# Bias vectors of folded weights: four column tiles and a second small matmul in place of full matmuls

## The chip, the cores and the metric

The kernel runs on one core of a Trainium2 chip. Its time is the device time of one execution in microseconds. The profile is one further execution, recorded by the hardware profiler. Engines are named as the profile names them: PE (matmuls) and PEld (weight loads), DVE (vector), ACT (activations), POOL (GpSimd), SP (issues most DMAs; a queue of an engine has a q behind its name).

## The reference

Two attention layers over a float32 image batch x of 8 x 512 x 32 x 32, so 8 images of 512 channels and 1024 tokens. Cut to what matters:

```python
# layer 0: eight heads of 64 channels, quantised q, k, v
h = group_norm(xf, gn_w, gn_b)                       # 32 groups
qkv = einsum('oc,bct->bot', qkv_w, h) + qkv_b
q, k, v = fake_quant(q), fake_quant(k), fake_quant(v)  # one scale each over the whole batch
w = softmax(einsum('bct,bcs->bts', q * scale, k * scale))
a = einsum('bts,bcs->bct', w, v)
x = xf + einsum('oc,bct->bot', proj_w, a) + proj_b
# layer 1: one head of 512 channels
t = group_norm(x, gn_w, gn_b) as tokens
q, k, v = t @ wq.T + bq, t @ wk.T + bk, t @ wv.T + bv
out = softmax(q @ k.T / sqrt(512)) @ v
x = x + out @ wp.T + bp
```

The kernel applies a norm's scale to x and leaves the norm's bias out of x. What that bias would have added after a linear layer is a constant vector, W times the norm's bias, and is added to the layer's own bias. Those vectors are what the change is about. The weights and biases are inputs, so they have to be computed on the chip in each execution.

## The kernel before

**First phase, about 0 to 628 us.** For each image b, x is loaded (`x`), normalised by DVE, and q, k, v are computed on PE with the weights `wqkv` (tiles `qkps` and `vps` in PSUM), evicted with their bias, tracked for minimum and maximum, and stored to DRAM (`q_d`, `k_d`, `v_d`). Image 0 is computed plainly; images 1 to 7 by a scheme of seven half-size products in place of eight (`qk_block`, `v_block`), for which sums of weights and tokens are kept. Here PSUM is one pool of eight banks (`one`).

The bias of q, k and v is made by `bias(i)`: `gbb` holds the norm's bias widened to 128 equal columns for each of the CC = 4 blocks e of 128 input channels. Four f32 matmuls with `gbb[:, e]` as weights and `wqkv[:, e, 512 columns]` as moving operand accumulate in one bank, in which all 128 rows are then equal: the vector lies along a row. For v that is the form wanted (`vb`). For q and k the vector is wanted by channel, one number per partition: `by_channel` multiplies each 128 x 128 block by the identity on DVE and sums each row (`qkb`). The three groups stand among image 0's matmuls: `bias(0)` after the third of its four channel blocks, `bias(1)` after the first k product, `bias(2)` after the first v product.

**Between the phases,** from the extrema of all images come the quantisation scales (`ext`, `exa` on POOL, `scl`, `rcp`, `bhi`). Meanwhile `fold()` starts on PE: it multiplies Wq by Wk and Wv by Wp of layer 1 (`wn`, loaded by `load_folded` into the tiles of tags h and v), 16 matmuls each, into `wa` and `wm`.

**Attention of image 0, from about 642 us.** A unit is a pair of heads, half of the 1024 queries and one block of 128 keys: two `st` matmuls, one exp on ACT (`pt`, six buffers), one sum `acc` on DVE, two `av` matmuls in column tiles of 64. A pair has 16 units, an image 64. At the end of a pair `row_sums` sums `acc` over the partitions with four column tiles of 32 (`sm`). The next pair's q, k and v are reloaded through `raw` (two buffers, SP queue) and quantised by DVE.

`fold()` is a generator; each step yields a weight, and the loop around it lets attention advance in proportion:

```python
for w in fold():
    folded += w
    while pos < (folded - F_FIRST) * A_IMAGE / F_FOLD:
        advance()
```

After the eight product steps come the bias steps. `gb` (for the scores of layer 1) is the folded Wq'Wk times layer 1's norm bias plus Wk' times bq; `ob` (for its output) is the folded Wv'Wp times the norm bias plus Wp' times bv, plus bp. For each, `weigh` runs two groups of four full matmuls into one bank `fold_b`: one over the folded matrix (`wa` or `wm`), one over `wn`, with `wide` (three biases, widened to 128 columns) as weights; then `by_channel`. Here the bank comes from a pool of two (`bank`). All matmuls are kept in program order on PE by `mm` (L96); on the other engines a scheduler orders the instructions when the kernel is built.

**The rest,** from about 776 us: for each image projection (`pj`), norm and layer 1, interleaved with the next image's attention.

Of the kernel before, what the change touches and what calls it, by code (L numbers as in the profile page):

```python
# [9 lines left out]
F32 = mybir.dt.float32  # L10
# [3 lines left out]
ALU = mybir.AluOpType  # L14
AX = mybir.AxisListType

P = 128
B, C, HH, WW = 8, 512, 32, 32
T = HH * WW
CC = C // P  # L20
# [3 lines left out]
PAIRS = HEADS // 2  # L24
# [16 lines left out]
V_GN0W, V_GN0B, V_PB0, V_GN1W, V_GN1B, V_BQ, V_BK, V_BP, V_BV, V_QKB = range(0, 40, 4)  # L41
# [3 lines left out]
WP0, WQ1, WK1, WV1, WP1, NQ1, NK1, NV1 = range(8)  # L45
# [3 lines left out]
def attn_pair_kernel(  # L49
# [9 lines left out]
    nc = tc.nc  # L59
# [10 lines left out]
    vec = const.tile([P, V_N], F32, name="vec")  # L70
    nc.scalar.dma_start(vec, vecs)
    ones = const.tile([P, P], F32, name="ones")
    nc.vector.memset(ones, 1.0)
    mhalf = const.tile([P, CC], F32, name="mhalf")
    nc.gpsimd.memset(mhalf, -0.5)

# [96 lines left out]
    with ExitStack() as fast:  # L173
# [7 lines left out]
        def bank(name):  # L181
            return ps_o.tile([P, 512], F32, tag="o", name=name)
# [35 lines left out]
        rs_d = [dram.tile([4, 512], F32, tag=f"rs{n}", name=f"rs_d{n}") for n in range(B * PAIRS)]  # L218
        rs1_d = [dram.tile([4, P], F32, tag=f"rs1{n}", name=f"rs1_d{n}") for n in range(B * NH)]

        def weigh(ps, terms):


            n = len(terms) * CC
            for i, (w, wide) in enumerate(terms):
                for e in range(CC):
                    mm(
                        ps.rearrange("p (a n) -> p a n", a=2), lhsT=wide[:, e, :], rhs=w(e),
                        start=(i == 0 and e == 0), stop=(i * CC + e == n - 1),
                    )  # L230
                yield 4.0

        def widen(dst, col):
            for e in range(CC):
                nc.vector.tensor_scalar(
                    dst[:, e, :], ones, vec[:, col + e : col + e + 1], None, ALU.mult
                )

        def by_channel(dst, ps):

            for e in range(CC):
                nc.vector.tensor_mul(ps[:, bass.ts(e, P)], ps[:, bass.ts(e, P)], ident)
            nc.vector.tensor_reduce(dst, ps.rearrange("p (e n) -> p e n", e=CC), AX.X, ALU.add)

        with tc.tile_pool(name="p1w", bufs=1) as p1w, tc.tile_pool(name="p1", bufs=3) as p1, tc.tile_pool(
            name="p1o", bufs=4
# [2 lines left out]
            def one(name):  # L249
                return ps_1.tile([P, 512], F32, tag="b", name=name)  # L250
# [216 lines left out]
            for i in range(2):  # L467
                nc.scalar.dma_start(vb[:, i, :], vbias[0:1, :].partition_broadcast(P))
            load_x(1)
            gbb = l1p.tile([P, CC, P], F32, tag="acc1", name="gbb")  # L470
            widen(gbb, V_GN0B)
            qkb = p1w.tile([P, 2 * PAIRS], F32, name="qkb")

            def bias(i):

                ps = one(f"bias{i}")
                w = wqkv[:, :, bass.ts(i, C)].rearrange("p e (a n) -> p e a n", a=2)
                for _ in weigh(ps, ((lambda e: w[:, e], gbb),)):
                    pass
                if i == 2:  # L480
                    for n in range(2):
                        nc.vector.tensor_add(vb[:, n, :], vb[:, n, :], ps)
                    return
                b4 = qkb[:, bass.ts(i, PAIRS)]
                by_channel(b4, ps)
                nc.vector.tensor_add(
                    b4, b4, vec[:, V_QKB + i * PAIRS : V_QKB + (i + 1) * PAIRS]
                )

            def qk_mm(b, ps, t, hf, cc):  # L490
# [8 lines left out]
            early = [[one(f"qkps_0_{t}_{hf}") for hf in range(NH)] for t in range(2)]  # L499
            for g in (*part, part[0], part[0], part[1]):  # L500
                next(g)
            then = iter((part[1], part[2], part[2], part[3], part[3]))
            for cc in range(CC):
                for t in range(2):
                    for hf in range(NH):
                        qk_mm(0, early[t], t, hf, cc)
                        if (cc, hf) in ((0, 1), (1, 0), (1, 1)):
                            next(next(then, iter(())), None)
                if cc == 2:
                    bias(0)  # L510
            load_x(2)
            ahead = prepare(1)
            more = weight_sums()
# [1 line left out]
            for t in range(2 * PAIRS):  # L515
                isk, j = divmod(t, PAIRS)
                if t < 2:
                    ps = early[t]
                else:
                    ps = [one(f"qkps_0_{t}_{hf}") for hf in range(NH)]  # L520
                    for hf in range(NH):
                        for cc in range(CC):
                            qk_mm(0, ps, t, hf, cc)
                if t == PAIRS:
                    bias(1)
                qk = p1o.tile([P, T], F32, tag="qk", name=f"qk1_0_{t}")
                mx, mn = (kmax, kmin) if isk else (qmax, qmin)
                for hf in range(NH):
                    nc.vector.tensor_scalar(
                        qk[:, bass.ts(hf, 512)], ps[hf], qkb[:, t : t + 1], None,  # L530
                        ALU.add, ALU.max, accum_out=column("kmax" if isk else "qmax", mx),
                    )
                nc.vector.tensor_reduce(mn[:, j : j + 1], qk, AX.X, ALU.min)
                nc.sync.dma_start((k_d if isk else q_d)[0][j], qk)
                if t > 0:
                    next(ahead, None)
            for t in range(NT):
                ps = one(f"vps_0_{t}")
                for cc in range(CC):
                    mm(  # L540
                        ps,
                        lhsT=hn[:, cc, bass.ts(t, P)],
                        rhs=wqkv[:, cc, 2 * C : 3 * C],
                        start=(cc == 0),
                        stop=(cc == CC - 1),
                    )
                if t == 0:
                    bias(2)
                vt = p1o.tile([P, 2, C], F32, tag="v2", bufs=3, name=f"v1_0_{t}")[:, 0, :]
                nc.vector.tensor_add(vt, ps, vb[:, 0, :])  # L550
                nc.vector.tensor_reduce(column("vmax", vmax), vt, AX.X, ALU.max)
                nc.vector.tensor_reduce(column("vmin", vmin), vt, AX.X, ALU.min)
                nc.sync.dma_start(v_d[0][:, t, :], vt)
                next(ahead, None)
                next(more, None)
# [733 lines left out]
        def fold():  # L1289


            wm = wm_tiles(0)

            def wa_rows(e):
                return wa[:, e // 2 : e // 2 + 3 : 2, e % 2, :]

            def wm_rows(e):
                return wm[e // 2][:, :, e % 2, :]

            for rows, lw, rw in ((wa_rows, NQ1, NK1), (wm_rows, NV1, WP1)):  # L1300
                for e in range(CC):
                    ps = bank(f"fold_{lw}_{e}")
                    for d in range(CC):
                        mm(
                            ps, lhsT=wn[lw][:, d, bass.ts(e, P)], rhs=wn[rw][:, d, :],
                            start=(d == 0), stop=(d == CC - 1),
                        )
                    nc.scalar.copy(rows(e), ps.rearrange("p (a n) -> p a n", a=2))
                    yield 4.0
            wide = l1p.tile([P, 3, CC, P], F32, tag="g", name="wide")  # L1310
            for i, col in enumerate((V_GN1B, V_BQ, V_BV)):
                widen(wide[:, i], col)

            def plain(i):
                w = wn[i].rearrange("p e (a n) -> p e a n", a=2)
                return lambda e: w[:, e]

            for i, (dst, w, w2) in enumerate(
                ((gb, wa_rows, plain(NK1)), (ob, wm_rows, plain(WP1)))
            ):  # L1320
                ps = bank(f"fold_b{i}")
                yield from weigh(ps, ((w, wide[:, 0]), (w2, wide[:, 1 + i])))
                by_channel(dst, ps)
            nc.vector.tensor_add(ob, ob, vec[:, V_BP : V_BP + CC])
            a11, a12, a21, a22, s1, s2, s4 = (wa[:, i] for i in range(7))
            tt(s1, a21, a22, ALU.add)
            tt(s2, s1, a11, ALU.subtract)
            tt(a21, a11, a21, ALU.subtract)
            tt(s4, a12, s2, ALU.subtract)
            (m11, m12), (m21, m22), (v1, v2), (v3, v4) = ([t[:, i] for i in range(2)] for t in wm)  # L1330
            tt(v1, m11, m12, ALU.subtract)
            tt(v2, m22, v1, ALU.subtract)
            tt(v3, m22, m12, ALU.add)
            tt(v4, m21, v2, ALU.subtract)
            for t, dst in zip(wm, wm_d):
                nc.sync.dma_start(dst, t)
# [24 lines left out]
        alone = True  # L1361
        att = attention()
        A_IMAGE = PAIRS * (NH * NT * 1.5 + 1.0)
        F_FOLD = 4.0 * (8 + 4)
        F_FIRST = 12.0
        pos, done = 0.0, 0
        dense = True
# [342 lines left out]
def _layout(i):  # L1710
# [12 lines left out]
    def col(v):  # L1723
# [14 lines left out]
            "L0_conv_proj_w", "L1_conv_wq", "L1_conv_wk", "L1_conv_wv", "L1_conv_wp",  # L1738
        )] + [wn(i[n]) for n in ("L1_conv_wq", "L1_conv_wk", "L1_conv_wv")]),
        "vecs": np.concatenate(vecs, axis=1),  # L1740
        "vbias": np.stack([qkv_b[:, 2].reshape(C), i["L1_conv_bv"]]),
    }


# [20 lines left out]
```

## Time and profile before

| | us |
|---|---|
| timed runs | median 2776.87 (2774.91 to 2778.79), three runs |
| profiled execution | 2774.02, span 2772.2 |
| PE busy in the span | 2714.3 (98%) |
| DVE busy | 1778.8 (64%) |
| ACT busy | 900.1 (32%) |
| `bias` matmuls, 24 passes | 592 ns each, from 33.5 to 91.9 |
| `fold_b` matmuls, 32 passes | 592 to 697 ns each, from 678.7 to 713.0 |

The profile lists an f32 matmul as two passes, so the twelve matmuls of `bias` are 24 rows. Passes are pipelined and overlap, so the time that a group takes from PE is read from the start of the group to the start of the next one, not from the sum of its durations. A row of the timeline reads: start, duration, engine, line, operation, output and inputs, shape, count, and in brackets how long the engine had been idle and who released it.

### The profile page before, as it was taken

To read this page: it belongs to the slowest core of one execution; us is meant where nothing else is said; L and a number is where in the kernel's file an instruction comes from. 1 tells how busy PE (TensorE), PEld (TensorE's weight loads), DVE (VectorE), ACT (ScalarE), POOL (GpSimd) and SP (SyncE) were. 2 spreads that over 40 slices of the span, in tenths; PEclk is the share of its full clock that TensorE was granted. 3 is DMA by queue.
4 is the path that set the end of the run, shared out by engine and by line. 5 is a ranking of instruction groups with operands and counts; after the bars stand their busy time and mean duration, and the time that the engine had idled before them with its cause. 6 is when DMAs were issued, how large, how long until landed. Compare 5 with 4: busy or idle time off the path is not lost.

```text
span 2772.2 us, 29206 instructions
## 1 busy us (share of the span) xinstructions
PE 2714.3 (98%) x11300; PEld 1646.7 (59%) x11300; DVE 1778.8 (64%) x2641; ACT 900.1 (32%) x1181; POOL 26.4 (1%) x28
## 2 busy tenths in 40 slices
PE   7999999999999999999999999999999999999998
PEld 3455555553236664665566556646664666467687
DVE  6666666547886667566766676666667566754544
ACT  0011111115644333433444244434443433443011
POOL 0000000000000000000000000000000000000000
PEclk9999999999999999999999999999999999999999
DMA  4323322135321232124212411231133124101301
GB/s 183 113 113 115 121 111 101 76 115 173 109 88 46 65 122 88 31 65 141 69 35 71 158 35 54 92 122 42 59 114 102 31 65 142 58 11 61 127 18 34
DMA packets 149094, 241.18 MB, mean 87 GB/s; under 512 B 24272, under 2 KB 89808, under 8 KB 147408
## 3 DMA queue, kind: packets, MB, share of 16 engines
q1 hardware_dynamic: 117424, 180.98, 19.6%
q10 hardware_dynamic: 31520, 58.23, 6.3%
q8 instruction: 90, 1.47, 0.2%
q14 instruction: 60, 0.49, 0.1%
HBM read 152.59 MB, written 86.28 MB: 86 GB/s over the span
## 4 chain that ended last, share of the span: by engine, by line
PE 77%; DVE 12%; DMA 6%; issue 2%; ACT 1%; POOL 1%; SPq 0%; ACTq 0%; DVEq 0%; POOLq 0%
PE qkps L96 12%; PE s L96 12%; PE av L96 12%; PE o L96 12%; PE pj L96 7%; PE v2ps L96 6%; PE vps L96 6%; PE g L96 5%; PE st L96 3%; DMA raw<-q_d 3%; DVE acc L752 3%; DVE acc L754 2%; PE sm L96 1%; ACT pt L743 1%; DVE h L145 1%
## 5 line engine op out<-in xcount | busy, mean ns | idle before, releaser
L743 ACT ACTIVATE pt<-st,esc 128x1024 f32<-128x1024 f32 x512 | 546.4, 1115 | 327.8 <-PE st L96 317.8
L96 PE MATMUL av<-pt,v 128*64 128x512 f32 x2048 | 476.5, 600 | 0.0
L752 DVE TENSOR_TENSOR acc<-acc,pt 128x1024 f32<-128x1024 f32 x254 | 310.6, 1223 | 117.6 <-ACT pt L743 108.1
L96 PEld LDWEIGHTS av<-pt,v 128*64 128x64 f32 x2048 | 132.0, 136 | 259.1 <-issue 258.7
L96 PE MATMUL s<-g,h 128*128 128x256 f32 x1024 | 236.5, 380 | 0.8
L96 PE MATMUL pj<-ao,wp 128*128 128x512 f32 x512 | 225.4, 596 | 7.5 <-DVE x L1126 3.6
L375 ACT ACTIVATE u<-qkps,qkb 128x512 f32<-128x512 f32 x84 | 57.7, 687 | 522.0 <-PE qkps L96 522.0
L96 PEld LDWEIGHTS s<-g,h 128*128 128x128 f32 x1024 | 193.5, 190 | 31.4 <-DVE v L1067 3.6
L96 PE MATMUL s<-g,sums 128*128 128x256 f32 x768 | 180.1, 384 | 4.1 <-DVE p L1082 3.4
L96 PEld LDWEIGHTS pj<-ao,wp 128*128 128x128 f32 x512 | 95.5, 190 | 131.4 <-issue 112.8
L754 DVE TENSOR_TENSOR acc<-acc,pt 128x1024 f32<-128x1024 f32 x130 | 158.5, 1219 | 21.7 <-ACT pt L743 18.0
L96 PE MATMUL o<-p,v 128*128 128x256 f32 x768 | 171.2, 379 | 0.0
L96 PEld LDWEIGHTS s<-g,sums 128*128 128x128 f32 x768 | 143.1, 190 | 36.9 <-issue 11.0
L96 PE MATMUL qkps<-x,wqkv 128*128 128x512 f32 x352 | 162.7, 606 | 2.3 <-DVE x L145 2.3
L96 PE MATMUL st<-q,k 64*128 64x512 bf16 x1024 | 157.0, 381 | 2.3 <-ACT pt L743 2.3
L96 PEld LDWEIGHTS o<-p,v 128*128 128x128 f32 x768 | 145.8, 190 | 20.1 <-issue 0.4
L96 PE MATMUL qkps<-sums,wa 128*128 128x512 f32 x336 | 153.3, 592 | 0.0
L96 PE MATMUL g<-h,wa 128*128 128x256 f32 x512 | 121.7, 385 | 12.2 <-DVE g L1025 11.4
L1082 DVE TENSOR_TENSOR p<-s,kept_u 128x512 f32<-128x512 f32 x90 | 61.8, 687 | 110.3 <-ACT kept_u L1049 102.2
L96 PEld LDWEIGHTS <-k 64*128 64x128 bf16 x1024 | 33.4, 94 | 164.7 <-issue 160.9
L96 PEld LDWEIGHTS g<-h,wa 128*128 128x128 f32 x512 | 94.7, 190 | 39.5 <-DVE g L1025 14.6
L96 PE MATMUL o<-g,vsum 128*128 128x256 f32 x512 | 117.2, 382 | 0.0
(210 smaller groups left out, 3358.5 us busy)
## 6 DMA issues: line engine op xcount, KB each, us to landing
x<-in_x_dram SPq DMA_DIRECT2D x32, 512.0 KB
raw<-q_d SPq DMA_DIRECT2D x32, 512.0 KB
raw<-k_d SPq DMA_DIRECT2D x32, 512.0 KB
raw<-v_d SPq DMA_DIRECT2D x32, 512.0 KB
rs<-rs_d SPq DMA_DIRECT2D x128, 128.0 KB
x_d<-h SPq DMA_DIRECT2D x64, 256.0 KB
x<-x_d ACTq DMA_DIRECT2D x64, 256.0 KB
out_dram<-x SPq DMA_DIRECT2D x64, 256.0 KB
```

Of the source, the lines that this page charges most:

```text
L96: ins = nc.tensor.matmul(*args, **kw).ins
L145: put(hf, lambda i=i, cc=cc, hf=hf: nc.vector.tensor_scalar(dst(cc, hf), src(cc, hf), mean[:, i : i + 1], rstd[:, i : i + 1], ALU.subtract ...
L375: nc.scalar.activation(dst, x, AF.Identity, bias=bias)
L743: nc.scalar.activation(pt, st, AF.Exp, scale=esc)
L752: later("sum", 0, lambda: nc.vector.tensor_add(acc, first, pt))
L754: nc.vector.tensor_add(acc, first, pt)
L1082: tt(dst, ps, u, ALU.add)
```

## The change

The vectors are computed in two steps. `weigh` runs the four blocks e as four matmuls of 32 weight columns each, each into its own 32 partitions of one bank (`wt`), so the four partial sums lie in four groups of 32 equal rows. ACT copies the bank to SBUF (`wsum` or `fold_room`). A second matmul with a constant `fourth` (4/128, a new tile) sums over the partitions: `by_channel` with four matmuls of one column (`wc`), which leaves the vector by channel, or `by_row` with one of 512 columns (`wr`) for v. The masking on DVE is gone.

In `fold()` the two steps over the folded matrices are gone. Instead DVE multiplies Wq and Wv of layer 1 with the norm's bias, loaded as a row (`gn1_row`, a third row of the input `vbias`), and sums (four instructions each, vector `z`), adds bq or bv, and widens that to 32 columns; `weigh` then runs over Wk or Wp alone. The second of the two `weigh` groups is followed by its reduction with nothing between. The weights of `fold()`'s steps sum to 34 in place of 48, so its steps fall differently between the units of attention.

```diff
+    fourth = const.tile([P, P], F32, name="fourth")
+    nc.gpsimd.memset(fourth, 4.0 / P)
...
-        def weigh(ps, terms):
-            n = len(terms) * CC
-            for i, (w, wide) in enumerate(terms):
+        def weigh(bank, room, w, wide, nm):
+            ps = bank(f"wt_{nm}")
+            for e in range(CC):
+                mm(
+                    ps[e * 32 : (e + 1) * 32, :], lhsT=wide[:, e, :], rhs=w(e),
+                    start=True, stop=True,
+                )
+            nc.scalar.copy(room, ps)
+            def by_channel():
+                tot = bank(f"wc_{nm}")[:, 0:CC]
                 for e in range(CC):
                     mm(
-                        ps.rearrange("p (a n) -> p a n", a=2), lhsT=wide[:, e, :], rhs=w(e),
-                        start=(i == 0 and e == 0), stop=(i * CC + e == n - 1),
+                        tot[:, e : e + 1], lhsT=room[:, bass.ts(e, P)], rhs=fourth[:, 0:1],
+                        start=True, stop=True,
                     )
-                yield 4.0
+                return tot
+            def by_row():
+                tot = bank(f"wr_{nm}")
+                mm(tot, lhsT=fourth, rhs=room, start=True, stop=True)
+                return tot
+            return by_channel, by_row
...
-        def by_channel(dst, ps):
-            for e in range(CC):
-                nc.vector.tensor_mul(ps[:, bass.ts(e, P)], ps[:, bass.ts(e, P)], ident)
-            nc.vector.tensor_reduce(dst, ps.rearrange("p (e n) -> p e n", e=CC), AX.X, ALU.add)
...
-                if cc == 2:
-                    bias(0)
+                if cc >= 2:
+                    next(bq, None)
...
-                if t == PAIRS:
-                    bias(1)
+                if t >= PAIRS - 1:
+                    next(bk, None)
+                if t == 2 * PAIRS - 1:
+                    next(bv)
...
+            row = l1p.tile([P, C], F32, tag="acc1", name="gn1_row")
+            nc.sync.dma_start(row, vbias[2:3, :].partition_broadcast(P))
+            wide = l1p.tile([P, 2, CC, 32], F32, tag="g", name="wide")
+            room = l1p.tile([P, C], F32, tag="rs1", name="fold_room")
+            for i, (w, w2, col) in enumerate(((NQ1, NK1, V_BQ), (NV1, WP1, V_BV))):
+                z = small.tile([P, CC], F32, tag="z", name=f"z{i}")
+                for e in range(CC):
+                    nc.vector.tensor_tensor_reduce(
+                        room, wn[w][:, e, :], row, 1.0, 0.0, ALU.mult, ALU.add,
+                        accum_out=z[:, e : e + 1],
+                    )
+                nc.vector.tensor_add(z, z, vec[:, col : col + CC])
+                widen(wide[:, i], z)
+            for i, (dst, w) in enumerate(((gb, NK1), (ob, WP1))):
+                by_channel, _ = weigh(
+                    bank, room, lambda e, w=w: wn[w][:, e, :], wide[:, i], f"f{i}"
+                )
+                yield 1.0
+                tot = by_channel()
+                if i == 0:
+                    nc.vector.tensor_copy(dst, tot)
+                else:
+                    nc.vector.tensor_add(dst, tot, vec[:, V_BP : V_BP + CC])
...
-        F_FOLD = 4.0 * (8 + 4)
+        F_FOLD = 4.0 * 8 + 2.0
```

More of the change, by code (lines that the diff above doesn't have):

```diff
@@ L235, in widen @@
                 nc.vector.tensor_scalar(
-                    dst[:, e, :], ones, vec[:, col + e : col + e + 1], None, ALU.mult
+                    dst[:, e, :], ones[:, 0:32], col[:, e : e + 1], None, ALU.mult
                 )
-        def by_channel(dst, ps):
-            for e in range(CC):
-                nc.vector.tensor_mul(ps[:, bass.ts(e, P)], ps[:, bass.ts(e, P)], ident)
-            nc.vector.tensor_reduce(dst, ps.rearrange("p (e n) -> p e n", e=CC), AX.X, ALU.add)
         with tc.tile_pool(name="p1w", bufs=1) as p1w, tc.tile_pool(name="p1", bufs=3) as p1, tc.tile_pool(
@@ L469, in attn_pair_kernel @@
             load_x(1)
-            gbb = l1p.tile([P, CC, P], F32, tag="acc1", name="gbb")
-            widen(gbb, V_GN0B)
+            gbb = l1p.tile([P, CC, 32], F32, tag="acc1", name="gbb")
+            widen(gbb, vec[:, V_GN0B : V_GN0B + CC])
             qkb = p1w.tile([P, 2 * PAIRS], F32, name="qkb")
             def bias(i):
[L476 to L479, printed above, removed]
+                by_channel, by_row = weigh(
+                    one, p1o.tile([P, 512], F32, tag="u4", bufs=1, name=f"wsum_{i}"),
+                    lambda e: wqkv[:, e, bass.ts(i, C)], gbb, f"{i}",
+                )
+                yield
                 if i == 2:
+                    tot = by_row()
                     for n in range(2):
-                        nc.vector.tensor_add(vb[:, n, :], vb[:, n, :], ps)
+                        nc.vector.tensor_add(vb[:, n, :], vb[:, n, :], tot)
                     return
-                b4 = qkb[:, bass.ts(i, PAIRS)]
-                by_channel(b4, ps)
                 nc.vector.tensor_add(
-                    b4, b4, vec[:, V_QKB + i * PAIRS : V_QKB + (i + 1) * PAIRS]
+                    qkb[:, bass.ts(i, PAIRS)], by_channel(),
+                    vec[:, V_QKB + i * PAIRS : V_QKB + (i + 1) * PAIRS],
                 )
@@ L501, in attn_pair_kernel @@
                 next(g)
+            bq, bk, bv = (bias(i) for i in range(3))
             then = iter((part[1], part[2], part[2], part[3], part[3]))
@@ L546, in attn_pair_kernel @@
                     )
-                if t == 0:
-                    bias(2)
+                next(bv, None)
                 vt = p1o.tile([P, 2, C], F32, tag="v2", bufs=3, name=f"v1_0_{t}")[:, 0, :]
@@ L1309, in fold @@
                     yield 4.0
[L1310 to L1324, printed above, removed]
+            row = l1p.tile([P, C], F32, tag="acc1", name="gn1_row")
+            nc.sync.dma_start(row, vbias[2:3, :].partition_broadcast(P))
+            wide = l1p.tile([P, 2, CC, 32], F32, tag="g", name="wide")
+            room = l1p.tile([P, C], F32, tag="rs1", name="fold_room")
+            sums_of = []
+            for i, (w, w2, col) in enumerate(((NQ1, NK1, V_BQ), (NV1, WP1, V_BV))):
[10 more added lines that the diff above has]
+                    bank, room, lambda e, w=w: wn[w][:, e, :], wide[:, i], f"f{i}"
+                )
+                yield 1.0
[4 more added lines that the diff above has]
+                    nc.vector.tensor_add(dst, tot, vec[:, V_BP : V_BP + CC])
             a11, a12, a21, a22, s1, s2, s4 = (wa[:, i] for i in range(7))
@@ L1740, in _layout @@
         "vecs": np.concatenate(vecs, axis=1),
-        "vbias": np.stack([qkv_b[:, 2].reshape(C), i["L1_conv_bv"]]),
+        "vbias": np.stack([qkv_b[:, 2].reshape(C), i["L1_conv_bv"], i["L1_conv_gn_b"]]),
     }
```

## The prediction

> **What bounds the kernel now.** I read the page's busy shares and its chain, then the busy time by stretch, then PE, DVE and SP in order of time where the bias matmuls stand, and last the chain of that part alone. Times "at 643" are microseconds from the start of the span of 2772.2.
>
> ```profile
> PE 2714.3 (98%) x11300; PEld 1646.7 (59%) x11300; DVE 1778.8 (64%) x2641; ACT 900.1 (32%) x1181; POOL 26.4 (1%) x28
> PE 77%; DVE 12%; DMA 6%; issue 2%; ACT 1%; POOL 1%; SPq 0%; ACTq 0%; DVEq 0%; POOLq 0%
> ```
>
> PE is the bound on average, but 12% of the chain is DVE and 6% DMA. By stretch (PE, PEld, DVE, ACT, POOL):
>
> ```profile
> 27.50:96.00 68.50, 68.50 (x160) 30.54 (x161) 51.68 (x110) 1.28 (x1) 1.95 (x2) 0.98 0.23 90
> 96.00:628.00 532.00, 530.51 (x1640) 308.82 (x1638) 334.29 (x650) 57.72 (x84) 6.05 (x6) 1.00 0.28 109
> 643.00:713.50 70.50, 70.50 (x278) 22.35 (x276) 56.30 (x64) 43.63 (x47) 0.00 (x0) 1.00 0.45 143
> 713.50:760.00 46.50, 42.49 (x205) 11.12 (x204) 42.58 (x48) 36.55 (x37) 0.00 (x0) 1.00 0.28 82
> ```
>
> The three `bias` groups lie in the first row, where PE never stops, and up to 628 it hardly does: what leaves PE there leaves the span. The four `fold_b` groups lie in the third row, PE full and DVE at 80%; in the fourth PE has 4 us of holes and DVE is at 92%. PE in order of time:
>
> ```profile
> 33.54 3.60 PE L96 MATMUL bias<-wqkv,gbb 128*128 128x512 f32 x8
> 36.97 11.32 PE L96 MATMUL qkps<-x,wqkv 128*128 128x512 f32 x26
> ...
> 708.88 1.06 PE L96 MATMUL sm<-acc,ones 128*32 128x512 f32 x8
> 709.88 3.70 PE L96 MATMUL fold_b<-wn_v,wide 128*128 128x512 f32 x8
> 713.51 0.61 PE L96 MATMUL st<-q,k 64*128 64x512 bf16 x4
> ```
>
> Start to start, four full f32 matmuls (eight passes) hold PE 36.97 - 33.54 = 3.43 us in the first phase and 713.51 - 709.88 = 3.63 us in attention. `sm` is already four column tiles of 32 side by side: 1.00 us. And the chain between 628 and 740, whose longest pieces are not PE's:
>
> ```profile
> 628.52 8.60 DMA k_d<-k
> 637.75 6.24 DMA raw<-v_d
> 673.03 5.80 DMA raw<-q_d
> 706.71 4.81 DMA raw<-q_d
> ```
>
> Beside PE runs a second chain there, of DVE and the reloads of `raw`, with next to no slack. So PE's gain there is not simply the span's.
>
> **What the Trainium skill says.** "TensorE: Matmul & The Clock Gate", Part 3, "Measured speedup vs the span model", has matmuls in different column groups run together: three tiles gave 2.38 times. The trace agrees: four `sm` tiles 1.00 us against 3.63, 3.6 times. "TensorEngine Tiling (Array Packing)", "Key Properties": changing the tiling mode drains the array. The trace has that inside `sm`'s 1.00 us, and the group after it loses nothing (3.63). The first page, "LDWEIGHTS (loading the stationary operand)", prices a load at its columns over 1.2 per ns, 107 ns for 128; the trace has 190 ns alone and 108 for 32 columns: the slope agrees, some 80 ns of latency come on top.
>
> **The change, part by part.**
>
> *First phase, PE.* Removed: three groups, 3 x 3.43 = 10.3. Added: three tile groups (`wt`) at the `sm` row's 1.00 = 3.0; for v one full matmul (`wr`), 3.43 / 4 = 0.86; for q and k four one-column matmuls each (`wc`). No row shows eight such weight loads in a row. Below: 8 x 107 ns = 0.9; above: 8 x 0.30, from `gps` on an idle PE, two passes in 0.59, = 2.4. I take 1.5, so 3.0 for both. Net 10.3 - 6.9 = 3.4. Each reduction waits for an ACT copy (0.59 as `wa<-fold`, once 1.28 for the table load, now first on ACT); in the built order 4 to 8 `qkps` or `vps` matmuls of 0.86 stand between, so it is hidden. A bias takes two of the eight PSUM banks in place of one, but `wt` leaves its bank to ACT at once, and PE wants no further bank for some 7 us. DVE loses the masking (two times 4 x 0.2 + 0.6) and evicts sooner; PE did not wait for that. The front order of DVE moves too: the normalisation of the second channel block comes about 1 us sooner by its rows (statistics of the fourth block fill a wait). PE stands 2.60 us for DVE before 27.22, so 0 to 1 of it; I take 0.5. Phase total 4 (2 to 5).
>
> *Hidden.* POOL: one memset (0.2, as `ident`) before `mhalf`, where POOL then sits idle 12. SP: `gn_row` stands before the store of `k_d` 3 and waits until `wt` 2 has read `gbb`, about 1 us after the store was ready; it and the v stores behind it only free buffers. DVE: eight multiply-and-sum instructions, each like `L350` 0.61 + 0.12 = 0.73. Four stand before the eviction that DVE waited 3.74 for at 620.56: 2.9 plus one add fit. Three, the add and four narrow widenings (together about 2.8) fit the 7.62 before `raw<-v_d` at 644.09. One stands ahead of the quantisation of `q_0` and `k_0` and waits for `wn_v`; its queue was empty at 636.6, the first half about 633, and PE needs `q_0` only at 642.5, when the first fold ends. The twelve wide widenings (0.2 each) go.
>
> *Attention of image 0.* Removed from PE: 4 x 3.63 = 14.5. Added: two `wt` 2.0, two `wc` 3.0. PE work falls by 9.5. With weights 34 for 48 the remaining folds sit later between units: after units 3, 7, 15 and 23 for 1, 3, 11 and 15. I walked PE, ACT, DVE and SP through the built order with these rows: st pair 0.53, av pair 1.87, exp 1.06, sum 1.13 to 1.23, quant 0.66, reload 4.4. Four things come out.
> 1. At the start `st` 2 and 3 now wait for the exps that the fold used to cover: about 1.6 of PE lost, and smaller waits later.
> 2. The DVE chain gains where the masking goes (1.94 at 699.7, 1.75 near 720) and where sums now fill its waits for `raw` (1.69 and 1.54).
> 3. A new wait: in the built order the last `wt`, `wc` follow each other. `wc` needs ACT's copy (0.8), and its bank (pool of two) only after DVE copies `gb`, which is queued on DVE behind four sums, the v quantisation and the `raw` reload. On PE everything stands behind it, first `st` of unit 36, then ACT. By the walk PE is ready at 707 and gets the bank at 709.4: a stand of 2 to 3.
> 4. `st` 36 starts at 710.6 for 713.5 (2.9 sooner), the sum over unit 36 at 712.2 for 720.6. Of those 8.4, 1.3 are two quants now still to do and 0.9 is masking that stood after it. After unit 36 DVE sets the pace: a pair of 16 units costs it 14 sums of 1.2, six quants of 0.66, 1.2 for `ao` and 0.25, 22.3 or 1.4 per unit, against PE's (0.53 + 1.87) / 2 = 1.2.
>
> So the stage ends about 7 sooner: at least 3 (PE's lead at unit 36, nothing more), at most 10 (all PE work, no stand). `h` now loads after the last `wt` of wn_h, some 5 later than before, and is first used at 776; the `wm_d` stores come later and are read an image later. From 776 the built order is the same, so the lead is kept.
>
> Sum: 4 + 7 = 11 against the profiled span 2772.2, whose run took 2774.02; the timed runs have a median of 2776.87 (2774.91 to 2778.79). The difference carries over to the median: 2766.
>
> **The rivals.**
> - *Attention gives its part back.* The DVE and reload chain (6.24, 5.80, 4.81 above) sets the stage's end and the new wait eats PE's lead; only the first phase and some masking remain: 4 + 1 = 5, time 2772, no measurable change. For it: the chain of 628 to 740. Against it: the chain itself loses 3.7 of masking and 3.2 of waits.
> - *All of PE's saving counts.* 3.4 + 9.5, weight loads at the low price (4 x 0.6 = 2.4), a front gain of 0.5: 15.8, time 2761. Against it: DVE at 92% in the fourth stretch.
> - *Slower: the tiles do not run side by side* with these operands, or each drains the array. Place: the five `wt` groups. A tile then costs a full matmul (0.86 or 0.91), 17.5 in place of 5; isolated `wc` cost 0.59 each, 9.4; `wr` 0.9 and the stand 3: 30.8 against 24.8 removed: 6 slower, 2783. It decides from a group of (5 + 11) / 5 = 3.2 us on. `sm` at 1.00, in f32 with 512 columns too, speaks against it.
> - *It does not do what it says:* the built order has the 32-row matmuls four by four, and the masking and `fold_b` groups are gone. Excluded.
>
> **How the numbers follow.** About 0.2% (5.5 us) is what a measurement of this kernel can tell from no change. Forecast 0.66, at 2766; part returned 0.16; all of it 0.11; slower 0.07. Faster is the forecast and all of it, 0.77; same 0.16; slower 0.07. The range reaches from all of PE's saving (2761) to between the returned case and no change (2774, a gain of 3: the low ends 2 + 3, less 2 for the spread of the runs); the slower case and a little of the returned one are outside.
>
> **What would show it.** Right: `wt` groups about 1.0 start to start, `wc` 0.9 to 2.4; PE without holes from 27 to 96, and the first fold about 4 sooner than 628.5; `q_0` and `k_0` ready before it ends; PE standing before the last `wc` with DVE or ACT as releaser; the first `pj` about 11 sooner than 776.0; from there to the end the same duration. Wrong: `wt` groups over 3 (the slower case); a fold that starts 4 sooner but a `pj` only 5 sooner (the returned case); a DVE wait on `wn_v` that PE's first fold does not cover; or a difference that arises after the first `pj`, for which I see no cause.

## The result and the profile after

The changed kernel took 2763.86 us (median of four runs, 2760.99 to 2766.21), the kernel before, run beside it, 2775.89 (four runs, 2773.35 to 2778.79). The ratio is 0.9956 (95% interval 0.9939 to 0.9973): 12.0 us sooner, where 11 were predicted. The profiled execution after (run of 2765.57) has a span of 2763.8, 8.4 shorter than the profiled span before. In the profiles the whole difference lies ahead of the first `pj`:

| us from the span's start | before | after | moved by |
|---|---|---|---|
| first fold matmul | 628.54 | 624.56 | 4.0 |
| first `pj` matmul | 776.00 | 767.72 | 8.3 |
| end | 2772.2 | 2763.8 | 8.4 |

I call the part between the first two "the stage"; it took 147.5 before and 143.2 after. The page's lines on busy time and on the chain:

```profile
PE 2706.2 (98%) x11318; PEld 1645.2 (60%) x11318; DVE 1776.9 (64%) x2636; ACT 902.0 (33%) x1186; POOL 26.6 (1%) x29
PE 79%; DVE 12%; DMA 4%; issue 2%; ACT 1%; POOL 1%; SPq 0%; DVEq 0%; ACTq 0%; POOLq 0%
```

PE lost 8.1 us of busy time. Busy time by stretch (PE, PEld, DVE, ACT, POOL, then the PE clock, the DMA share and GB/s), the first row moved to its new border:

```profile
27.50:91.50 64.00, 64.00 (x178) 28.39 (x178) 48.07 (x99) 1.75 (x3) 1.95 (x2) 0.97 0.26 97
...
643.00:713.50 70.50, 66.31 (x283) 20.49 (x281) 55.95 (x62) 42.48 (x47) 0.00 (x0) 0.94 0.42 141
713.50:760.00 46.50, 46.50 (x234) 12.30 (x232) 44.21 (x47) 40.63 (x42) 0.00 (x0) 1.00 0.31 92
```

The first phase is without holes, as before. Two things are new, both in the row from 643 us. PE, full before, now has 4.2 us of holes there, and its clock is 0.94. (I call a time in which PE does nothing and waits a "stand".) The row behind it has lost its holes in exchange. PE in order of time:

```profile
33.70 1.07 PE L99 MATMUL wt<-wqkv,gbb 128*32 128x512 f32 x8
34.69 3.70 PE L99 MATMUL qkps<-x,wqkv 128*128 128x512 f32 x8
38.23 0.95 PE L99 MATMUL wc<-fourth,wsum 128*128 128x1 f32 x8
39.04 13.98 PE L99 MATMUL qkps<-x,wqkv 128*128 128x512 f32 x32
...
640.25 0.39 PE L99 MATMUL st<-q,k 64*128 64x512 bf16 x2 [1.15 <-ACT pt L760]
641.25 0.39 PE L99 MATMUL st<-q,k 64*128 64x512 bf16 x2 [0.61 <-ACT pt L760]
641.58 5.40 PE L99 MATMUL fold<-wn_v 128*128 128x512 f32 x8
...
707.49 1.84 PE L99 MATMUL wc_f<-fourth,fold_room 128*128 128x1 f32 x8 [4.20 <-DVE gb L1349]
709.26 1.03 PE L99 MATMUL st<-q,k 64*128 64x512 bf16 x4
710.23 3.55 PE L99 MATMUL av<-pt,v 128*64 128x512 f32 x8
```

Start to start, a bias group now holds PE for 0.99 us (34.69 - 33.70) and its reduction for 0.81 (39.04 - 38.23). At 703 the stand that the prediction had as term 3 is there, with `gb` as releaser, 4.20 long. And what follows each stand is slow (start to start again): the fold group at 641.58 takes 5.33 where the others take 3.63, the `wc_f` at 707.49 takes 1.77 where the first took 0.98, the av pair behind it 3.48 for 1.87. PE's clock around the second of these stands (columns: PE busy, clock, DMA share, GB/s):

```profile
706.00:708.00 2.00, 0.51 (x3) 0.67 1.05 409
708.00:710.00 2.00, 2.00 (x11) 0.50 0.82 309
```

The clock is halved from the last microsecond of the stand on, and still at 0.62 from 712 to 714. DVE over the same time shows what `gb` was queued behind:

```profile
702.26 0.75 DVE L642 TENSOR_SCALAR raw<-raw,rcp 128x1024 f32<-128x1024 f32 x1 [2.05 <-DMA raw<-v_d]
...
706.05 1.22 DVE L769 TENSOR_TENSOR acc<-acc,pt 128x1024 f32<-128x1024 f32 x1
707.19 0.16 DVE L1349 COPY gb<-wc_f 128x4 f32<-128x4 f32 x1
```

The `wc_f` whose bank it empties was done at 702.3. The copy of four columns came 5 us later, after a wait for a reload, two quantisation passes and three sums.

### The profile page after: what moved, and what is told of

Same layout as the page of the kernel before. It is cut to its first block, busy times and chain, and to the rows that moved or that the text cites. A ratio compares the mean times of both kernels' runs of the same rounds, so it can differ in the third digit from the quotient of the medians.

```text
span 2763.8 us, 29246 instructions
## 1 busy us (share of the span) xinstructions
PE 2706.2 (98%) x11318; PEld 1645.2 (60%) x11318; DVE 1776.9 (64%) x2636; ACT 902.0 (33%) x1186; POOL 26.6 (1%) x29
## 4 chain that ended last, share of the span: by engine, by line
PE 79%; DVE 12%; DMA 4%; issue 2%; ACT 1%; POOL 1%; SPq 0%; DVEq 0%; ACTq 0%; POOLq 0%
PE av L99 13%; PE qkps L99 12%; PE s L99 12%; PE o L99 12%; PE pj L99 6%; PE v2ps L99 6%; PE vps L99 6%; PE g L99 6%; PE st L99 4%; DVE acc L769 3%; DMA raw<-q_d 2%; DVE acc L771 2%; ACT pt L760 1%; PE sm L99 1%; PE fold L99 1%
## 5 line engine op out<-in xcount | busy, mean ns | idle before, releaser
L99 PEld LDWEIGHTS s<-g,sums 128*128 128x128 f32 x768 | 143.2, 190 | 36.7 <-issue 11.0
```

The lines of the kernel that those rows point to most:

```text
L99: ins = nc.tensor.matmul(*args, **kw).ins
```

## The experiments

My theory after the result: the change is two separate gains, one by each part. The stage's gain is cut by two stands of PE (for the exps at 640, for `gb` at 703) and by the half clock behind each. Rivals: the stage is set by the exps, sums and reloads, so that a shorter stand only moves PE's wait; the gain is PE work alone and the stand costs nothing; the tiles are cheap for being narrow, not for running together. In the table, "fold" and "pj" are the starts of the first matmul of each in one profile; median and ratio are of the timed runs. Each ratio is against runs of the kernel before made beside that run (medians 2773.5 to 2775.9), so across rows the ratios are to be compared rather than the medians.

| run | fold | pj | stage | median | ratio (95%) |
|---|---|---|---|---|---|
| before | 628.54 | 776.00 | 147.5 | 2775.89 | |
| after | 624.56 | 767.72 | 143.2 | 2763.86 | 0.9956 (0.9939 to 0.9973) |
| first_alone | 624.69 | 773.67 | 149.0 | 2768.96 | 0.9975 (0.9965 to 0.9985) |
| fold_alone | 629.31 | 770.37 | 141.1 | 2769.30 | 0.9979 (0.9969 to 0.9988) |
| one_bank | 621.80 | 765.24 | 143.4 | 2762.62 | 0.9956 (0.9943 to 0.9969) |
| own_bank | 625.59 | 765.08 | 139.5 | 2758.94 | 0.9943 (0.9931 to 0.9955) |
| first14 | 626.49 | 764.65 | 138.2 | 2757.72 | 0.9939 (0.9924 to 0.9955) |
| own_first14 | 624.94 | 760.95 | 136.0 | 2754.77 | 0.9926 (0.9913 to 0.9939) |
| fill | 625.06 | 767.38 | 142.3 | 2762.48 | 0.9957 (0.9944 to 0.9970) |
| one_group | 630.45 | 775.80 | 145.4 | 2773.55 | 0.9996 (0.9990 to 1.0002) |
| no_products | 621.50 | 765.44 | 143.9 | 2763.14 | 0.9960 (0.9947 to 0.9974) |
| warm | 622.11 | 757.01 | 134.9 | 2755.77 | 0.9929 (0.9915 to 0.9943) |

**One part at a time.** `first_alone` keeps the old `weigh`, `widen` and `by_channel` for the fold and F_FOLD at 48 (the last lines of the edit, against the changed kernel):

```diff
...
-        F_FOLD = 4.0 * 8 + 2.0
+        F_FOLD = 4.0 * (8 + 4)
```

> Only the first phase is changed; the fold, its bias and its pace are those of before. Milestones: the first fold matmul started at 628.54 us before and 624.56 after, the first pj group at 776.00 and 767.72. Two separate gains: fold at about 624.6, first pj at about 772.0 (the stage between takes its old 147.5 us), end 4 us under before. If the new pace of the attention needs the earlier start of the fold, the first pj comes elsewhere than 772.

`fold_alone` keeps the old bias of image 0 (one place of several):

```diff
...
-                if cc >= 2:
-                    next(bq, None)
+                if cc == 2:
+                    bias(0)
...
```

> Only the fold's bias and its pace are changed; the first phase is that of before. Two separate gains: first fold matmul at about 628.5 us, first pj at about 771.7 (the stage takes 143.2 us, as after), end 4 to 4.5 us under before, with the stand before the second wc and the halved clock behind it. If the stand came from the first phase's shift alone, it is missing here and the stage is shorter than 143.2.

Measured: the first fold starts at 624.69 and 629.31, the medians are 6.1 and 5.8 us under the 2775.06 that the kernel before took beside them; together 11.9, and the whole change gave 12.0. By the intervals the two are 4.2 to 9.7 and 3.3 to 8.6, so the gains are separate and, within these, add up. The stand is there with the second part alone, 3.46 us before the last `wc_f`, so it does not come from the earlier start. The stages are 149.0 (expected 147.5) and 141.1 (143.2): one profile resolves a stage to about 1.5 to 2 us, no better.

**The wait taken away: first try.** `one_bank` puts both channel sums into one tile, which `by_channel` now takes as an argument:

```diff
...
                 yield 1.0
-                tot = by_channel()
+                if i == 0:
+                    both = bank("wc_f")
+                tot = by_channel(both[:, i * CC : (i + 1) * CC])
```

> The after kernel with both channel sums in one PSUM tile (columns 0 to 3 and 4 to 7), so that the second wc waits for ScalarE's copy alone and no longer for the copy to gb on VectorE. Wait theory: the 4.20 us stand falls to 0.8 to 1.2, the clock stays at 1.00 around it, and the first pj comes 4 to 6 us sooner than after (762 to 764 us). Rival that the sums and exps set the stage: the stand is found again before the next st or av, and the first pj stays within 1 us of 767.7.

A miss, by the edit and not by a theory. The stand stayed:

```profile
705.12 1.84 PE L99 MATMUL wc_f<-fourth,fold_room 128*128 128x1 f32 x8 [5.06 <-DVE gb L1352]
```

Writing columns 4 to 7 still waits for the reader of columns 0 to 3 in the built program, so this run says nothing on what the wait costs.

**The wait taken away: second try.** `own_bank` writes each reduction into the first columns of its own `wt_f` bank, from which ScalarE has already copied:

```diff
-            def by_channel():
-                tot = bank(f"wc_{nm}")[:, 0:CC]
+            def by_channel(own=False):
+                tot = (ps if own else bank(f"wc_{nm}"))[:, 0:CC]
...
-                tot = by_channel()
+                tot = by_channel(own=True)
```

> The after kernel with the fold's channel sums written into the first columns of their own wt_f bank, which ScalarE has copied out by then: the second wc waits for that copy alone. The edit of one_bank had kept the wait on gb, this one has none in its built form. Measured from the first fold matmul to the first pj (147.5 us before, 143.2 after). Wait theory: the stand of 4.20 us falls to about 1, the halved clock behind it goes or shortens, the stage takes 137 to 139 us. Rival that exps and sums set the stage: PE stands later instead, the stage stays at 142 to 144 us.

PE of this run, where the second reduction (first row) now bears the name `wt_f`:

```profile
704.27 1.05 PE L99 MATMUL wt_f<-fourth,fold_room 128*128 128x1 f32 x8 [0.76 <-ACT fold_room L234]
705.25 0.80 PE L99 MATMUL st<-q,k 64*128 64x512 bf16 x4
705.98 3.39 PE L99 MATMUL av<-pt,v 128*64 128x512 f32 x8
```

The stand went from 4.20 to 0.76 and the stage to 139.5, just above the 137 to 139 of the wait theory and below the 142 to 144 of its rival. The half clock stayed in part (av pair 3.32 start to start), with only two short stands shortly before it, 0.58 for the sum `acc` at 699.9 and 0.76 for the copy. In this profile the fold group behind the stands for the exps also ran at full clock (3.63); the run `fill` below shows why that hardly counts.

**The stands for the exps.** F_FOLD at 34 also lets four `st` tiles follow each other at 638.5 to 641.6, and the third needs a bank that the first exp frees. `first14` changes only where attention begins:

```diff
-        F_FIRST = 12.0
+        F_FIRST = 14.0
```

> The after kernel with F_FIRST 14 instead of 12: two st tiles instead of four stand between the fourth and the fifth fold group, as before the change. If the halved clock at 642 to 646 us comes from the stands of 1.15 and 0.61 us for the exps: these stands go, the fifth fold group takes 3.6 to 3.7 us instead of 5.33, and the first pj comes about 3 us sooner than after as far as the later stand before the second wc stays as it is (4.2 us). Rival that the stage is set by the exps and sums: fold group at 3.6 us, but the first pj unchanged within 1 us.

```profile
640.96 3.70 PE L99 MATMUL fold<-wn_v 128*128 128x512 f32 x8
...
697.92 1.83 PE L99 MATMUL wc_f<-fourth,fold_room 128*128 128x1 f32 x8 [2.72 <-DVE gb L1349]
```

The fold group stands behind the second `st` tile again, as before the change. The stands for the exps are gone and the group takes 3.63 (644.59 - 640.96, the next start). The stage is 5.0 us shorter than after, more than the expected 3; the shifted order also shortened the later stand, to 2.72. The rival that exps and sums set the stage had the first `pj` unchanged within 1 us, and falls for this part.

**Both together.** `own_first14` holds both edits:

> own_bank and F_FIRST 14 together. Two separate losses: the stage from the first fold matmul to the first pj takes about 134 us (first14 had 138.2 with a stand of 2.72 us and some 2.5 us of halved clock behind it; both go), the end some 6 us under after. If one cause lies behind both, or the exps become the bound, it stays at 137 to 138 us.

The stage takes 136.0, 2 us more than expected, and no instruction in it runs at half clock; the stands left before the first `pj` are 1.3 for the exps, 1.0 for `acc` and 0.8 for the copy. The median is 2754.77 (2750.24 to 2758.82), 9 us under after, and the runs of the two do not overlap: a version that beats both kernels. For `own_bank` and `first14` alone the timed runs don't show it clearly, since their intervals overlap that of after.

**Stand or clock.** `fill` leaves the wait and puts PE to work in it, with three matmuls whose result is not used:

```diff
-            def by_channel():
+            def by_channel(fill=0):
+                for _ in range(fill):
+                    mm(ps, lhsT=fourth, rhs=room, start=True, stop=True)
...
-                tot = by_channel()
+                tot = by_channel(fill=3 * i)
```

> The after kernel with three idle 128x512 matmuls (0.9 us each) into the finished wt_f bank ahead of the second wc; their result is not used. The wait on the copy to gb stays as long as it was, but PE is at work in most of it. If the halved clock comes from the stand: full clock at 706 to 714 us of after, wc_f at 0.98 instead of 1.77, av pair 1.87 instead of 3.48, stage from the first fold matmul to the first pj at about 140.4 us instead of 143.2. If the clock falls for another reason, or the later work is not bound by PE: 143.

```profile
704.37 2.84 PE L99 MATMUL wt_f<-fold_room,fourth 128*128 128x512 f32 x6 [0.76 <-ACT fold_room L234]
707.11 1.05 PE L99 MATMUL wc_f<-fourth,fold_room 128*128 128x1 f32 x8
708.10 0.61 PE L99 MATMUL st<-q,k 64*128 64x512 bf16 x4
708.63 1.94 PE L99 MATMUL av<-pt,v 128*64 128x512 f32 x8
```

Behind the filled wait `wc_f` takes 0.99, `st` 0.53, the av pair 1.87, all at full clock. In all six profiles with a stand of 2.7 to 5.1 us in this place `wc_f` took 1.77, so the half clock came with the stand, as far as one profile shows it.

On the clock's worth the run missed: 142.3 for 140.4, though in this profile the fold group behind the exps was at full clock too (3.63 for the 5.33 of after). Together the half clock had cost PE's rows 4.5 us in after (1.70 + 0.79 + 0.44 + 1.61). Fill has none of it, and yet its stage is only 0.9 shorter and its ratio the same. The second pair's `sm` shows where the time went, first in fill, then in after:

```profile
698.57 1.05 PE L99 MATMUL sm<-acc,ones 128*32 128x512 f32 x4
700.58 1.05 PE L99 MATMUL sm<-acc,ones 128*32 128x512 f32 x4 [0.96 <-DVE acc L771]
701.56 1.05 PE L99 MATMUL wc_f<-fourth,fold_room 128*128 128x1 f32 x8
```

```profile
699.50 1.82 PE L99 MATMUL sm<-acc,ones 128*32 128x512 f32 x8
701.25 1.05 PE L99 MATMUL wc_f<-fourth,fold_room 128*128 128x1 f32 x8
```

Counted from the first fold matmul, fill reaches this `sm` 1.4 us sooner (73.5 for 74.9) and leaves it 0.2 sooner (76.5 for 76.7): PE ran ahead and waited for the sums. Start to start the last three `sm` groups of the stage take 2.99, 2.07 and 3.52 in fill, 1.75, 1.00 and 1.73 in after, 4.1 us more. So the sums set a floor close below, and nearly all of the clock's time was not to be had: on the clock the rival, that the sums set the stage, holds. The fair partner of own_bank is this run, with the same full clock at the exps: 139.5 for 142.3, so about 2.8 us of stage for the wait itself.

**Do the column tiles run together?** `one_group` adds the four 32-column matmuls up in one column group and reduces over its 32 partitions (the reductions' own lines are left out here):

```diff
...
-                    ps[e * 32 : (e + 1) * 32, :], lhsT=wide[:, e, :], rhs=w(e),
-                    start=True, stop=True,
+                    ps[0:32, :], lhsT=wide[:, e, :], rhs=w(e),
+                    start=(e == 0), stop=(e == CC - 1),
...
```

> The after kernel with its four 32-column matmuls added up in one column group (start on the first, stop on the last, 32 partitions reduced) instead of side by side. If the column tiles run at the same time: a wt group takes about 3.4 us instead of 0.99, five groups add 12 us, end at about the time of before. Rival that 32 columns are cheaper than 128 by themselves: a wt group stays near 1 us and the time near that of after.

```profile
30.98 3.62 PE L99 MATMUL wt<-wqkv,gbb 128*32 128x512 f32 x8
34.53 3.70 PE L99 MATMUL qkps<-x,wqkv 128*128 128x512 f32 x8
```

3.55 us a group against 0.99 side by side, and with five such groups the time is that of before (ratio 0.9996). Narrow weights by themselves save nothing; running together is the whole gain of the `wt` groups.

**The part moved to DVE.** `no_products` widens `bq` and `bv` alone; it leaves out the norm's bias through Wq and Wv:

```diff
-                    nc.vector.tensor_tensor_reduce(
-                        room, wn[w][:, e, :], row, 1.0, 0.0, ALU.mult, ALU.add,
-                        accum_out=z[:, e : e + 1],
-                    )
-                nc.vector.tensor_add(z, z, vec[:, col : col + CC])
-                widen(wide[:, i], z)
+                widen(wide[:, i], vec[:, col : col + CC])
```

> The after kernel without the eight multiply-sums on VectorE and the two additions behind them: it leaves out layer 1's norm bias through Wq and Wv, and the columns are widened from the vectors of bq and bv alone. If VectorE's share is hidden, as the prediction had it: the stage from the first fold matmul to the first pj stays at 143 us within 1.5 and the time at that of after (ratio 0.995 to 0.996). If VectorE sets the stage: the eight products of about 0.68 us (5.4 us) come out of it, first at the waits for the v tiles, and the stage falls to 138 to 141.

Stage 143.9, ratio 0.9960, against 143.2 and 0.9956: the eight products cost nothing that can be measured. (On its first fold at 621.50 see the next run.)

**A stand in the first phase.** In all runs so far PE stands 2.60 us ahead of the last small norm matmul of image 0, and the profiles differ in the clock behind it. PE's busy time and clock in two stretches of first14, and below of one_bank:

```profile
30.00:32.00 2.00, 2.00 (x4) 0.50 0.02 6
32.00:34.00 2.00, 2.00 (x3) 0.50 0.00 0
```

```profile
30.00:32.00 2.00, 2.00 (x12) 1.00 0.03 10
32.00:34.00 2.00, 2.00 (x5) 1.00 0.00 0
```

The kernels differ only in the fold, and yet one has half the clock of the other here. Their first fold starts at 626.49 and 621.80. `warm` is own_first14 with two matmuls in that stand whose result is not used:

```diff
+            def warm():
+                spare = one("warm")
+                for _ in range(2):
+                    mm(spare, lhsT=gavg, rhs=wqkv[:, 0, 0:512], start=True, stop=True)
+                next(part[3])
+                yield
...
-            then = iter((part[1], part[2], part[2], part[3], part[3]))
+            then = iter((part[1], part[2], part[2], part[3], warm()))
```

> own_first14 with two idle 128x512 matmuls (0.9 us each at full clock) in the stand of 2.60 us ahead of the last small norm matmul of image 0, at 24 to 26 us; their result is not used. If that stand halves the clock of the 2 to 7 us behind it: the clock is 1.00 from 26 us on in every run, the first fold matmul starts at 621.5 to 623.5 (621.8 was the one run that kept its clock, 624 to 626.5 the others), the median falls by 1.5 to 3 us under own_first14's 2754.8, and the spread of the runs gets smaller. If the clock falls there for another reason, the first fold matmul stays at 624 to 626.

```profile
23.79 1.88 PE L99 MATMUL warm<-wqkv,gavg 128*128 128x512 f32 x4
26.55 0.38 PE L99 MATMUL gps_a<-gd_a,gavg 128*128 128x1 f32 x2 [0.88 <-DVE gd_a L138]
```

The clock held: 1.00 behind the stand, a mean of 0.999 in each of the five timed runs (0.997 to 0.999 in own_first14), and the first fold at 622.11. The median did not follow: 2755.77 (2751.08 to 2756.84) against 2754.77, ratios 0.9929 and 0.9926. That half of the expectation failed. From the first `pj` to the end all twelve profiles take between 1990.8 and 1998.1 us, with the waits of `g` and `pj` for DVE different each time, and this profile has 1997.3. Whether a gain of 2 us at 27 us is lost there or only drowned in that spread stays open.

## Why the prediction was right, and where it was not

**The sum.** Predicted 11 = 4 + 7. The timed runs gave 12.0, and 6.1 and 5.8 for the parts alone. The profiled pair gave 8.3 = 4.0 + 4.3 to the first `pj`. The likeliest case was nearest, and the range held the result. That 12.0 came so close to 11 is in part luck: the profiled pair moved the first `pj` by 8.3, not by the 11 that the prediction named as its sign, and the rest lies in the spread of the runs (last paragraph of this section).

**First phase: 4 predicted, 4.0 in the profiled pair, by errors that cancelled.** The removed 10.3 stands. `wt` took 0.99, 1.00 and 0.99, `wr` 0.86, as taken. `wc` took 0.81 and 0.82 instead of 1.5, below even the bound of 0.9. I had read its price from single loads on an idle PE; eight in a row overlap. So the rows give 10.3 - 5.5 = 4.8. Of this some 0.6 is lost again because the group behind each of the six small groups is about 0.1 longer: the `qkps` matmuls between `wt` and `wc` take 3.54 (38.23 - 34.69), for 3.43 when nothing small stands before them. This also corrects a reading of the prediction: a group behind a tiled one does lose a little. The 3.63 of attention, where it saw no loss, is itself 0.2 above the 3.43 of groups in a row. The 0.5 from DVE's front order did not come: the stand of 2.60 is in this profile as in that of before. The pair can be compared because each of the two has 3.4 us of half clock behind that stand; other profiles have none or 6.8.

**Hidden work.** As predicted: the four products on `wn_h` fit the wait of 3.74 (0.60 of it is left after), and no_products shows no cost of the whole, within what it can resolve.

**Rivals on the tiles.** The slower case needed groups of 3.2 us or more; they took 0.99. one_group, in which they run one after another, shows that the price of that case for a `wt` group was right (3.55).

**The stage: 7 predicted, 4.3 in the profile. This is the step that failed, in its size.** Term 1, `st` 2 and 3 waiting for the exps, was put at 1.6 and measured 1.76 (1.15 + 0.61). Term 3, the stand for `gb`, was in the right place with the right releaser, but 4.20 instead of 2 to 3. With the first phase's 4.0 added back, so on the times of before, PE was ready at 707.3, as walked (707), and the bank came at 711.5 instead of 709.4. The reload that DVE waits for is 0.5 of that:

```profile
697.31 4.93 DMA raw<-v_d
```

This is from the chain; 4.4 was taken. Where the rest of the delay arose is open. What the walk did not have at all is the clock: it priced each PE row at full clock, and the stands that it correctly put in made the rows behind them slow, by 1.70 on the fold group, 0.79 on `wc_f`, 0.44 on `st` and 1.61 on the av pair. Only the `wc_f` counts for the start of unit 36: it took 1.77 where the walk had 1.2 from bank to `st`. The 1.70 of the fold group was gone by the second `sm`, as fill shows. So `st` of unit 36 came at 709.26, on the times of before 713.2; term 4 had 710.6, and 713.51 is where it stood before. The excess of 2.6 is 2.1 of a later bank and 0.6 of clock. Of the lead of 2.9 that the walk gave PE at unit 36, 0.3 was left.

The stage still gained 4.3 because PE, delayed, met almost no waits later: it had 3.2 us of holes from 715 to 740 before the change and none after. Term 4 had DVE set the pace from unit 36 on; in this profile PE is full there (46.50 of 46.50 us in the row from 713.50). The runs support this reading in its parts. The stand: own_bank, stage 139.5. The order at the start: first14, 138.2. Both: 136.0. The clock's cause: fill. What fill also shows is that the rival "attention gives its part back" is partly right, since a PE that gets ahead soon waits for the sums, as term 4 said.

**From the first `pj` on.** "The same duration" held for the profiled pair, 1996.2 and 1996.1. The spread of 7 us over twelve profiles says that such closeness is luck, and that the 3.6 us between the profiled gain (8.4) and that of the medians (12.0) needs no cause in the change.

## What to carry to other kernels

When several small matmuls are added up, lay them in column tiles side by side and sum the tiles with one further small matmul: here four took 0.99 us for 3.43, and the sum 0.81. If the second step follows the first with nothing between, look for whatever frees its bank, and give it a bank that an engine with little queued frees, here ScalarE: a copy of four columns queued behind other VectorE work held PE for 4.2 us. A stand of PE can cost its length plus the half clock that follows it; whether it does depends on what waits next. Here, with the sums close behind, taking the half clock away brought under 1 us of 4.5. Fill a stand with useful matmuls by the order of the work first: moving the start of attention by one constant was worth as much as the bank.

## What was not expected of the hardware

- PE's clock halves after stands shorter than I would have counted. The Trainium skill, "TensorE: Matmul & The Clock Gate", Part 1, has the clock fall after at least one idle window of about 3.4 us, and says that the window runs freely, so that it varies from run to run. The variation agrees with these traces, the length does not: behind the stand of 2.60 us in the first phase the clock was at 0.5 in eight of eleven profiles, for some 3 to 7 us, and stayed at 1.00 in three. Behind two stands of 1.15 and 0.61 us with PE at work between, the fold group took 5.33 us in four profiles and 3.63 in three. Stands of 0.58 and 0.76 us were followed by half clock in own_bank, stands of 0.96 and 0.76 in fill were not. Between 20 and 800 us each stretch of half clock in the twelve profiles lasts about 3.4 us, twice that, or (once) three times.
- In kernels with the same first phase the first fold matmul starts between 621.5 and 626.5 us. Up to 6.8 us of half clock, so 3.4 us of lost work, are most of that, nearly as much as the first part of the change was worth.
- Eight one-column f32 passes with eight weight loads of 128 x 128 took 0.81 us, 0.10 each, where a single pair on an idle PE showed 0.59. The prediction's lower bound, 0.9, was close.
